# Four row tiles transposed within the weights' product, in four banks, and a bias product summed over chunks on VectorE

## The chip, the cores and the metric

The kernel runs on one core of a Trainium2 chip. The metric is the device time in microseconds (us) of one execution. Engines are named as the profile names them: PE is TensorE, DVE is VectorE, ACT is ScalarE, POOL is GpSimd, SP is SyncE, which here only issues DMA transfers.

## The reference

Two layers over a graph of N = 3327 rows and D = 512 columns. Everything is 32-bit floating point.

```
h  = relu(layernorm(x))
q, k, v = h Wq^T + bq, h Wk^T + bk, h Wv^T + bv
a  = q k^T / sqrt(512) + adj + adj
x  = x + softmax(a) v

h  = relu(layernorm(x))
A2 = adj + I,   s = diagonal(A2)^(-1/2)
x  = x + relu((s A2 s) (A2 h W1^T))
```

Only the preparation of the first layer's scores matters for the change. The kernel doesn't form q and k one by one: with M = Wq^T Wk / sqrt(512) and u = Wk^T bq / sqrt(512), the scores are (h M + u) h^T, up to a term that is constant along a row and drops out of the softmax.

## The kernel before

Rows are padded to 26 tiles of 128. The program is written with a tile framework that orders each engine's instructions by its own planner from the order of the text and adds the waits; from the score stage on an order written by hand is forced on PE, DVE, POOL and SP (`in_order`). On each engine instructions run in that order. So what moves in the text need not move equally far on every engine.

**Loading (L286 to L293).** Wq and Wk come in four chunks of 128 rows each, Wq on SP's queue and Wk on ACT's. From the second chunk on, an x tile follows on each of the two queues. The bias `bq_sb`, 128 x 4 values, comes after them on SP's queue (L293); all later x tiles, the adjacency blocks `g` and the stores of finished rows also go on SP's queue.

**The weights' product (L298 to L314).** Eight products of zeros into the bank `idle` (L302) run on PE while the first weights come. Then M: four banks `ps[r]`, 0 to 3, each summed over the four chunks `c`, so 16 products of 128x128 by 128x512 (L306); in 32-bit floating point each is two passes in the profile. ACT scales them out of PSUM in eight pieces (L311), and DVE forms one sum (L312) and three differences (`four_differences`, L181 to L183) that the products below need.

**Row tiles (`h_transposed`, L316).** The tiles are taken in four packs, `PACKS` = (0,4), (4,3), (7,3), (10,3), in the order `TURN` = 1, 2, 0, 3. A pack of n covers n tiles of the upper half and n of the lower half of the rows, so the first pack that is worked on has six tiles. For each tile: load x (`load_x`, L275, 11 buffers in turn), statistics on DVE (`norm`, L194 to L198), the power -1/2 on POOL (L200), the shift `nb` on DVE (L204), `ht` on ACT (L323, four buffers in turn), a store of `ht` (L324), four transposes on PE into one bank `tp` (L327), and the copies: all four blocks by ACT for an upper tile (L330), or two by ACT (L332) and two sums by DVE (L333, L334) for a lower one. `tp_bank` (L229) takes banks 6 and 7 in turn. After a pack's last tile DVE forms two more sums over the pack (L335, L336).

**The bias product (L370 to L375).** `pu`, in bank 4, holds Wk^T bq: for each of the four column blocks `r`, four products over the chunks `c`, each with a 128x128 block of Wk as weights and one column of `bq_sb` as the moving operand. DVE scales it into `u` (L375), which ACT adds to the projected rows (L352).

```
for r in range(DC):
    for c in range(DC):
        nc.tensor.matmul(pu[:, r : r + 1], w_k[c // 2][:, c % 2, r * P : (r + 1) * P], bq_sb[:, c : c + 1],
                         start=c == 0, stop=c == DC - 1)
```

**Projection (`project_q`, L338).** For a pack, two chains of seven products each (`Chain`, L231) between the blocks of M and the pack's `hp`, in the banks X (0, 1), Y (2, 3) and Z (4, 5), L347; results go to `qs` by ACT (L352) and DVE (L355) and are stored to DRAM (L362). The transposes of the next pack are woven in between by the planner.

**Afterwards** come the scores (L454), with the adjacency and the exponentials, and then the large products over the rows (L813 and others) of both layers. Their text is the same before and after.

Of the kernel before, what the change touches and what calls it, by code (L numbers as in the profile page):

```python
# [12 lines left out]
ALU = mybir.AluOpType  # L13
AX = mybir.AxisListType

P = 128
# [31 lines left out]
def graph_layers_kernel(  # L48
# [28 lines left out]
    nc = tc.nc  # L77
    N = out.shape[0]
    NP, D = x.shape
    DC = D // P  # L80
    NT = NP // P
    scale = 1.0 / math.sqrt(D)
    E = D // 2
# [22 lines left out]
    def half(k, shape, name):  # L106
        return arena.tile(shape, F32, name=name, tag=f"half{k}")

    def bank(k, name):
        return banks.tile([P, BW], F32, name=name, tag=f"bank{k}")  # L110
# [35 lines left out]
    ones = const.tile([P, 1], F32, name="ones")  # L146
# [9 lines left out]
    bq_sb = const.tile([P, DC], F32, name="bq_sb")  # L156
# [20 lines left out]
    def four_differences(b, first=0):  # L177

        if first == 0:
            yield nc.vector.tensor_sub(b[4], b[0], b[1])  # L180
        yield nc.vector.tensor_add(b[5], b[3], b[4])  # L181
        yield nc.vector.tensor_sub(b[6], b[1], b[3])
        yield nc.vector.tensor_sub(b[7], b[2], b[5])  # L183
# [7 lines left out]
    def norm(src):  # L191

        st = small.tile([P, 6], F32, name="st")
        nc.vector.bn_stats(st, src)  # L194
        mv = small.tile([P, 2], F32, name="mv")
        nc.vector.bn_aggr(mv, st)
        ve = small.tile([P, 1], F32, name="ve")
        nc.vector.tensor_scalar(ve, mv[:, 1:2], EPS, None, op0=ALU.add)  # L198
        rstd = small.tile([P, 1], F32, name="rstd")
        nc.gpsimd.tensor_tensor(rstd, ve, mhalf, op=ALU.pow)  # L200

        def bias():
            nb = small.tile([P, 1], F32, name="nb")
            nc.vector.scalar_tensor_tensor(nb, mv[:, 0:1], -1.0, rstd, op0=ALU.mult, op1=ALU.mult)  # L204
            return nb

        return rstd, bias
# [6 lines left out]
    TURN = (1, 2, 0, 3)  # L214
# [10 lines left out]
    def psum_ring(*ks):  # L225
        turn = itertools.cycle(ks)
        return lambda name: bank(next(turn), name)

    x_bank, y_bank, z_bank, tp_bank = psum_ring(0, 1), psum_ring(2, 3), psum_ring(4, 5), psum_ring(6, 7)  # L229
# [43 lines left out]
    def load_x(i, queue=nc.sync):  # L273
        xt = x_ring([P, D], "xt")
        queue.dma_start(xt, x[ROW[i] * P : (ROW[i] + 1) * P])  # L275
        return xt
# [3 lines left out]
    def blocks(slots, name):  # L280

        return [b[:, k] for b in (half(j, [P, 2, 2, E], name) for j in slots) for k in range(2)]

    w_q, w_k = ([half(k, [P, 2, D], name) for k in slots] for name, slots in (("wq", (0, 1)), ("wk", (2, 3))))

    first = {}  # L286
    for c in range(DC):
        for w, src, queue in ((w_q, wq, nc.sync), (w_k, wk, nc.scalar)):
            queue.dma_start(w[c // 2][:, c % 2], src[c * P : (c + 1) * P])
        if c > 0:  # L290
            for (_, i), queue in zip(order[2 * c - 2 : 2 * c], (nc.sync, nc.scalar)):
                first[i] = load_x(i, queue)
    nc.sync.dma_start(bq_sb, bq)  # L293
    M = blocks(range(4, 8), "M")
    u = const.tile([P, DC], F32, name="u")

# [3 lines left out]
    idle = bank(5, "idle")  # L300
    for _ in range(8):
        nc.tensor.matmul(idle[:, :P], zero, zero, start=True, stop=True)  # L302
    ps = [bank(k, "mm") for k in range(DC)]
    for c in range(DC):
        for r in range(DC):
            nc.tensor.matmul(ps[r], w_q[c // 2][:, c % 2, r * P : (r + 1) * P], w_k[c // 2][:, c % 2],  # L306
                             start=c == 0, stop=c == DC - 1)
    for r in range(DC):
        for z in range(2):
            turned = -scale if r < 2 and z == 0 else scale  # L310
            nc.scalar.mul(M[2 * (r // 2) + z][:, r % 2], ps[r][:, z * E : (z + 1) * E], turned)  # L311
    nc.vector.scalar_tensor_tensor(M[4], M[0], -1.0, M[1], op0=ALU.mult, op1=ALU.subtract)  # L312
    for _ in four_differences(M, 1):
        pass  # L314

    def h_transposed(k):  # L316

        a, n = PACKS[k]
        for _, i in (o for o in order if o[0] == k):
            xt = first.pop(i) if i in first else load_x(i)  # L320
            rstd, bias = norm(xt)
            ht = n_ring([P, D], "ht")
            nc.scalar.activation(ht, xt, AF.Relu, bias=bias(), scale=rstd)  # L323
            nc.sync.dma_start(rowd[0][ROW[i]], ht)  # L324
            pt = tp_bank("tp").rearrange("p (c e) -> p c e", c=DC)
            for c in range(DC):
                nc.tensor.transpose(pt[:, c], ht[:, c * P : (c + 1) * P], ident)  # L327
            w = slice((i % HALF - a) * P, (i % HALF - a + 1) * P)
            if i < HALF:
                nc.scalar.copy(hp[k][:, 0:2, :, w], pt.rearrange("p (a c) e -> p a c e", a=2))  # L330
            else:
                nc.scalar.copy(hp[k][:, 2, :, w], pt[:, 2:4])  # L332
                nc.vector.tensor_add(hp[k][:, 3, :, w], hp[k][:, 2, :, w], pt[:, 0:2])  # L333
                nc.vector.tensor_add(hp[k][:, 5, :, w], hp[k][:, 0, :, w], pt[:, 0:2])  # L334
        nc.vector.tensor_add(hp[k][:, 4], hp[k][:, 3], hp[k][:, 0])  # L335
        nc.vector.tensor_add(hp[k][:, 6], hp[k][:, 1], hp[k][:, 4])  # L336

    def project_q(k):  # L338
        a, n = PACKS[k]
        w = n * P  # L340

        qs = [half(8 + j, [P, 2, BW], "qs") for j in range(4)]

        def chain(o):
            def product(ps, name, start):
                for c in range(2):
                    nc.tensor.matmul(ps[:, :w], M[B[name]][:, c, o * P : (o + 1) * P], hp[k][:, A[name], c],  # L347
                                     start=start and c == 0, stop=c == 1, skip_group_check=True)

            def first(j, ps, sign):  # L350
                d = 2 * (j % 2) + o
                nc.scalar.activation(qs[j][:, o, :w], ps[:, :w], AF.Identity, bias=u[:, d : d + 1], scale=float(sign))  # L352

            def more(j, ps):
                nc.vector.tensor_add(qs[j][:, o, :w], qs[j][:, o, :w], ps[:, :w])  # L355

            def last():
                if o == 1:
                    for j in range(4):
                        y, z = divmod(j, 2)  # L360
                        i = ROW[y * HALF + a] * P
                        nc.sync.dma_start(qd[:, 2 * z : 2 * z + 2, i : i + w], qs[j][:, :, :w])  # L362

            Chain(product, first, more, last)

        for o in range(2):
            chain(o)

    h_transposed(TURN[0])
    pu = bank(4, "pu")  # L370
    for r in range(DC):
        for c in range(DC):
            nc.tensor.matmul(pu[:, r : r + 1], w_k[c // 2][:, c % 2, r * P : (r + 1) * P], bq_sb[:, c : c + 1],
                             start=c == 0, stop=c == DC - 1)
    nc.vector.tensor_scalar(u, pu[:, :DC], scale, None, op0=ALU.mult)  # L375
    for k, then in itertools.zip_longest(TURN, TURN[1:]):
        if then is not None:
            h_transposed(then)
        project_q(k)


# [170 lines left out]
    with in_order(*(e.engine for e in (nc.vector, nc.tensor, nc.gpsimd, nc.sync))):  # L552
# [9 lines left out]
        k = len(steps)  # L562
# [459 lines left out]
    def number_of(g, r, s, t):  # L1022
        return ((g * len(ORDER) + r) * 2 + s) * len(every) + t
# [5 lines left out]
    for g in range(3):  # L1029
        for n, r in enumerate(ORDER):  # L1030
            for t, e in enumerate(every):
                k = number_of(g, n, 0, t)
# [9 lines left out]
    for n, job in enumerate(jobs):  # L1042
        k = k0 + n * (k1 - k0) // len(jobs)
# [15 lines left out]
    k = number_of(0, 5, 1, 2)  # L1059
# [6 lines left out]
    k = number_of(1, 5, 1, 2)  # L1066
# [9 lines left out]
    for (n, s, t), its in {  # L1076
# [4 lines left out]
        for i, when in zip(its, (between, within)):  # L1081
            if i is not None:
                k = number_of(2, n, s, t)
# [8 lines left out]
    k = number_of(1, 4, 0, 0)  # L1092
# [480 lines left out]
```

## Time and profile before

| what | value |
|---|---|
| time, median of 3 runs | 2179.59 us (2177.32 to 2180.01) |
| profiled execution: its own time | 2178.22 us |
| profiled execution: span | 2176.4 us |
| PE busy | 2163.2 us (99%) |
| DVE busy | 1664.5 us (76%) |
| ACT busy | 238.4 us (11%) |
| first product of the score stage (L454) starts | 115.99 us |

The time of an execution is somewhat longer than its span, which runs from the first to the last instruction. PE busy counts pipelined products with modelled ends; a busy PE can still be working at a lower clock, which the profile shows as PEclk. In the chain of waits the last instruction is followed back to what released it, so its pieces add up to the span. In lists of groups, `x` is a count of records: two for a product in 32-bit floating point, one for a transpose. Line numbers are those of the kernel before.

### The profile page before, as it was taken

To read this page: it belongs to the slowest core of one execution; us is meant where nothing else is said; L and a number is where in the kernel's file an instruction comes from. 1 tells how busy PE (TensorE), PEld (TensorE's weight loads), DVE (VectorE), ACT (ScalarE), POOL (GpSimd) and SP (SyncE) were. 2 spreads that over 40 slices of the span, in tenths; PEclk is the share of its full clock that TensorE was granted. 3 is DMA by queue.
4 is the path that set the end of the run, shared out by engine and by line. 5 is a ranking of instruction groups with operands and counts; after the bars stand their busy time and mean duration, and the time that the engine had idled before them with its cause. 6 is when DMAs were issued, how large, how long until landed. Compare 5 with 4: busy or idle time off the path is not lost.

```text
span 2176.4 us, 21093 instructions
## 1 busy us (share of the span) xinstructions
PE 2163.2 (99%) x6424; PEld 1197.1 (55%) x6424; DVE 1664.5 (76%) x3250; ACT 238.4 (11%) x363; POOL 49.0 (2%) x60
## 2 busy tenths in 40 slices
PE   9999999999999999999999999999999999999998
PEld 6555555455555555555454555555666655555555
DVE  6369888888886698886778778887676667778686
ACT  5312111121110000000000000000011100000011
POOL 2000000000000000000111000000000000000000
PEclk9999999999999999999999999999999999999999
DMA  8568888889989899888787889986646468756685
GB/s 290 177 222 308 294 298 287 294 290 310 321 290 298 291 377 331 287 296 304 259 304 263 308 277 370 320 303 219 207 145 200 142 202 276 254 188 212 218 305 194
DMA packets 300374, 583.68 MB, mean 268 GB/s; under 512 B 34518, under 2 KB 168028, under 8 KB 300252
## 3 DMA queue, kind: packets, MB, share of 16 engines
q1 hardware_dynamic: 265102, 512.76, 69.4%
q10 hardware_dynamic: 35150, 69.48, 8.7%
q8 instruction: 53, 0.87, 0.2%
q14 instruction: 69, 0.57, 0.1%
HBM read 414.28 MB, written 167.85 MB: 267 GB/s over the span
## 4 chain that ended last, share of the span: by engine, by line
PE 95%; DVE 3%; DMA 1%; issue 1%; ACT 0%; POOL 0%; DVEq 0%; POOLq 0%
PE p L813 54%; PE Y L454 13%; PE Z L454 7%; PE p L805 5%; PE p L905 4%; PE pw L966 3%; PE X L454 3%; PE Y L347 2%; PE Z L347 1%; PE mm L306 1%; DMA part<-sum 1%; PE tp L327 1%; DVE part L173 1%; PE pt L995 1%; PE X L347 0%
## 5 line engine op out<-in xcount | busy, mean ns | idle before, releaser
L813 PE MATMUL p<-part,b 128*128 128x448 f32 (+1 forms) x3528 | 1261.5, 513 | 0.3 <-DVE part L174 0.2
L813 PEld LDWEIGHTS p<-part,b 128*128 128x128 f32 x3528 | 668.1, 190 | 534.7 <-issue 284.7
L454 PE MATMUL Y<-qt,hp 128*128 128x448 f32 (+1 forms) x832 | 308.2, 513 | 0.3 <-DVE g L466 0.3
L173 DVE TENSOR_TENSOR part<-part 128x896 f32<-128x896 f32 (+1 forms) x252 | 257.0, 1020 | 65.7 <-DMA part<-p 24.0
L454 PEld LDWEIGHTS Y<-qt,hp 128*128 128x128 f32 x832 | 157.7, 190 | 134.3 <-issue 72.3
L454 PE MATMUL Z<-qt,hp 128*128 128x384 f32 (+1 forms) x416 | 162.5, 513 | 0.0
L175 DVE TENSOR_TENSOR part<-part,part 128x448 f32<-128x448 f32 (+1 forms) x219 | 129.5, 591 | 14.9
L174 DVE TENSOR_TENSOR part<-part,part 128x448 f32<-128x448 f32 (+1 forms) x219 | 129.4, 591 | 7.2
L805 PE MATMUL p<-part,b 128*128 128x448 f32 (+1 forms) x336 | 124.2, 513 | 0.0
L454 PEld LDWEIGHTS Z<-qt,hp 128*128 128x128 f32 x416 | 78.8, 190 | 67.4 <-issue 37.2
L458 DVE SCALAR_TENSOR_TENSOR g<-g,Y 128x384 f32<-128x384 f32 (+1 forms) x156 | 91.5, 587 | 31.3 <-PE Y L454 28.6
L805 PEld LDWEIGHTS p<-part,b 128*128 128x128 f32 x336 | 63.7, 190 | 53.5 <-issue 31.2
L841 ACT COPY part<-p 128x384 f32<-128x384 f32 (+1 forms) x33 | 16.6, 502 | 657.5 <-PE p L813 542.1
L454 PE MATMUL X<-qt,hp 128*128 128x384 f32 (+1 forms) x208 | 81.1, 512 | 0.0
L461 ACT ACTIVATE g<-g 128x768 f32<-128x768 f32 (+1 forms) x48 | 43.0, 896 | 347.8 <-DVE g L458 278.6
L905 PE MATMUL p<-w,ct 128*128 128x512 f32 x136 | 61.8, 594 | 0.5 <-DVE part L917 0.5
L842 DVE TENSOR_TENSOR part<-p,part 128x384 f32<-128x384 f32 (+1 forms) x33 | 19.3, 585 | 51.6 <-PE p L813 50.9
L454 PEld LDWEIGHTS X<-qt,hp 128*128 128x128 f32 x208 | 39.5, 190 | 33.1 <-issue 19.3
L200 POOL TENSOR_TENSOR rstd<-ve,mhalf 128x1 f32<-128x1 f32 x52 | 43.0, 830 | 567.9 <-DVE ve L198 538.7
L966 PE MATMUL pw<-w,rows 128*128 128x256 f32 x208 | 53.6, 380 | 0.8 <-DVE rows L956 0.8
L896 DVE TENSOR_TENSOR job<-job 128x896 f32<-128x896 f32 (+1 forms) x52 | 52.9, 1018 | 0.0
L466 DVE TENSOR_TENSOR g<-g,Z 128x384 f32<-128x384 f32 (+1 forms) x52 | 30.5, 586 | 26.8 <-PE Z L454 26.4
(176 smaller groups left out, 1697.6 us busy)
## 6 DMA issues: line engine op xcount, KB each, us to landing
part<-sum SPq DMA_DIRECT2D x104, 448.0 KB, 5.0
part<-p SPq DMA_DIRECT2D x91, 448.0 KB, 6.0
part<-sum SPq DMA_DIRECT2D x104, 384.0 KB, 3.7
part<-p SPq DMA_DIRECT2D x91, 384.0 KB, 4.4
part<-in_adjT_dram SPq DMA_DIRECT2D x78, 448.0 KB, 4.9
b<-row SPq DMA_DIRECT2D x234, 128.0 KB, 4.7
part<-in_adjT_dram SPq DMA_DIRECT2D x78, 384.0 KB, 3.5
g<-in_adjT_dram SPq DMA_DIRECT2D x52, 448.0 KB, 4.4
```

The costliest lines, as they stand in the source:

```text
L173: yield nc.vector.tensor_add(o[:, 0:2], g[:, 0:4:3], g[:, 1:2].to_broadcast([P, 2, g.shape[-1]]))
L174: yield nc.vector.tensor_add(o[:, 2], o[:, 1], g[:, 0])
L175: yield nc.vector.tensor_add(o[:, 3], o[:, 2], g[:, 2])
L200: nc.gpsimd.tensor_tensor(rstd, ve, mhalf, op=ALU.pow)
L347: nc.tensor.matmul(ps[:, :w], M[B[name]][:, c, o * P : (o + 1) * P], hp[k][:, A[name], c], start=start and c == 0, stop=c == 1, skip_group ...
L454: nc.tensor.matmul(ps[:, :wd], h_of(self.t, name, k), qt[B[name]][:, k], start=start and k == 0, stop=k == 1, skip_group_check=True)
L458: nc.vector.scalar_tensor_tensor(a[n], a[n], 2.0, ps[:, :wd], op0=ALU.mult, op1=ALU.add if sign > 0 else ALU.subtract)
L805: yield nc.tensor.matmul(ps[("p2", "p3", "p4", "p8")[k]][:, :w], b[:, z], a[:, 0, y], start=k == 3, stop=True)
L813: yield nc.tensor.matmul(ps[r][:, :w], b[:, i], m, start=self.t == 0, stop=self.t == PAIRS - 1 and r in ("p1", "p5", "p6", "p7"))
L896: nc.vector.tensor_add(self.a, self.a, self.b)
L905: nc.tensor.matmul(ps, cts[s][y][d][:, k * P : (k + 1) * P], w[d], start=d == 0, stop=d == DC - 1)
L966: nc.tensor.matmul(ps, a, W[B[name]][:, c], start=new and c == 0, stop=c == 1, skip_group_check=True)
```

## The change

Three things change, all in the first stretch of the program.

The six tiles of the first pack are now made by a generator. Its first four tiles are drawn in the text between chunk 2 and chunk 3 of the weights' product, the other two after M and its differences. For this pack the transposes take the banks 6, 7, 4, 5 in turn; the later packs keep 6 and 7.

The bias is first multiplied into the rows of Wk on DVE: `weighed`, 128x512, is the sum over the chunks of a chunk of Wk times its column of the bias, one instruction for each chunk. Then four products of a 128x128 block of `weighed` with the column `ones` give `pu`, now in bank 0, in place of sixteen.

The bias is loaded on ACT's queue after the second chunk of Wk, in place of SP's queue after the last chunk.

```diff
@@ loading
     for c in range(DC):
         for w, src, queue in ((w_q, wq, nc.sync), (w_k, wk, nc.scalar)):
             queue.dma_start(w[c // 2][:, c % 2], src[c * P : (c + 1) * P])
+        if c == 1:
+            nc.scalar.dma_start(bq_sb, bq)
         if c > 0:
             for (_, i), queue in zip(order[2 * c - 2 : 2 * c], (nc.sync, nc.scalar)):
                 first[i] = load_x(i, queue)
-    nc.sync.dma_start(bq_sb, bq)
@@ h_transposed
-    def h_transposed(k):
+    def h_transposed(k, tp_bank=tp_bank):
...
                 nc.vector.tensor_add(hp[k][:, 5, :, w], hp[k][:, 0, :, w], pt[:, 0:2])
+            yield
         nc.vector.tensor_add(hp[k][:, 4], hp[k][:, 3], hp[k][:, 0])
@@ the weights' product; the scaling into M and the differences follow it as before
     ps = [bank(k, "mm") for k in range(DC)]
+    begun = h_transposed(TURN[0], psum_ring(6, 7, 4, 5))
+    weighed = half(12, [P, D], "weighed")
     for c in range(DC):
+        if c == DC - 1:
+            for _ in itertools.islice(begun, 4):
+                pass
+        if c == 0:
+            nc.vector.tensor_scalar(weighed, w_k[0][:, 0], bq_sb[:, 0:1], None, op0=ALU.mult)
+        else:
+            nc.vector.scalar_tensor_tensor(weighed, w_k[c // 2][:, c % 2], bq_sb[:, c : c + 1], weighed,
+                                           op0=ALU.mult, op1=ALU.add)
         for r in range(DC):
             nc.tensor.matmul(ps[r], w_q[c // 2][:, c % 2, r * P : (r + 1) * P], w_k[c // 2][:, c % 2],
                              start=c == 0, stop=c == DC - 1)
@@ after M and its differences
-    h_transposed(TURN[0])
-    pu = bank(4, "pu")
+    for _ in begun:
+        pass
+    pu = bank(0, "pu")
     for r in range(DC):
-        for c in range(DC):
-            nc.tensor.matmul(pu[:, r : r + 1], w_k[c // 2][:, c % 2, r * P : (r + 1) * P], bq_sb[:, c : c + 1],
-                             start=c == 0, stop=c == DC - 1)
+        nc.tensor.matmul(pu[:, r : r + 1], weighed[:, r * P : (r + 1) * P], ones, start=True, stop=True)
     nc.vector.tensor_scalar(u, pu[:, :DC], scale, None, op0=ALU.mult)
```

## The prediction

> **What bounds the kernel now.** I read the page first, then the waits of TensorE, then the chain of waits over the first 60 us, then the table by stage.
>
> ```profile
> PE 2163.2 (99%) x6424; PEld 1197.1 (55%) x6424; DVE 1664.5 (76%) x3250; ACT 238.4 (11%) x363; POOL 49.0 (2%) x60
> ...
> PE 95%; DVE 3%; DMA 1%; issue 1%; ACT 0%; POOL 0%; DVEq 0%; POOLq 0%
> ```
>
> TensorE is busy 99% of the span and holds 95% of the chain that ended last. The change touches only the first 30 us, so the question is what TensorE loses there: passes that can go, waits, and passes at a lower clock. Its waits over the whole run are few:
>
> ```profile
> PE tp L327 <- ACT hp L330: 0.7, 1, 0.7
> PE tot L507 <- DVE acc L510: 0.6, 1, 0.6
> ```
>
> The longest is in the stretch that is changed; all others lie after 600 us, but for 0.14 us at 54.8. After 31 us TensorE runs almost without a hole, so a microsecond saved before that should reach the end. The chain of the first stretch (start, length, what; x counts passes):
>
> ```profile
> 4.92 14.82 PE mm L306 x32
> 19.74 0.87 PE tp L327 x8
> 20.61 3.47 PE pu L373 x32
> 24.08 0.91 PE tp L327 x4
> 24.99 0.02 issue
> 25.01 0.59 ACT hp L330
> 25.61 0.04 issue
> 25.65 1.97 PE tp L327 x8
> 27.62 1.47 PE Y L347 x2
> 29.09 0.85 PE tp L327 x4
> 29.95 1.16 PE Y L347 x2
> 31.10 0.65 PE X L347 x2
> 31.75 0.87 PE tp L327 x8
> ```
>
> To be seen here: the 16 one-column products `pu` cost 3.47 us; then 0.66 us of waiting for ACT's copy; and the same shapes cost twice as much from 24 to 31 us as after it (eight transposes 1.97 against 0.87, two passes of a product 1.47 against 0.65). The table by stage (us, PE busy, PEld, DVE, ACT, POOL, PEclk, DMA share, GB/s) says why:
>
> ```profile
> 23.00:24.00 1.00, 1.00 (x11) 1.00 (x11) 1.00 (x4) 0.00 (x0) 0.00 (x0) 1.00 0.95 283
> 24.00:25.00 1.00, 0.97 (x5) 0.57 (x4) 0.53 (x4) 0.00 (x0) 0.00 (x0) 0.51 0.64 225
> 27.00:28.00 1.00, 1.00 (x4) 0.72 (x4) 1.00 (x8) 1.00 (x2) 0.00 (x0) 0.50 0.86 301
> 31.00:32.00 1.00, 1.00 (x7) 0.69 (x6) 0.06 (x1) 0.75 (x2) 0.55 (x1) 1.00 0.00 0
> ```
>
> The granted clock (PEclk) halves at about 24.0 and returns at about 30.9.
>
> **What the Trainium skill says.** "TensorE: Matmul & The Clock Gate", Part 1: the clock is set by TensorE's activity in free-running windows of 3413 ns; a window without it brings half clock. The trace agrees in length: 24.0 to 30.9 is two windows, and the one before them, 20.6 to 24.0, holds nothing but `pu`. The same page, Part 4, says that transposes do not count as activity in the same way; that fits the second window, 24.0 to 27.4, which held only transposes and the wait. No view shows how little activity is too little: 27.4 to 30.9, about 70% product passes, brought full clock back.
>
> **The change, part by part.** The program's new order on each engine can be read without running it; from the thirteenth row tile's transposes on, TensorE's order is the old one.
>
> 1. *`pu` from 16 products to 4.* 32 passes at 3.47/32 = 0.108 us become 8: 3.47 - 0.87 = **2.60 us less**, all on TensorE's path.
>
> 2. *The wait at 24.99 goes: 0.66 us less.* With two banks in turn the fifth tile needs the third's, whose copy on ACT had only begun. Now the first four tiles have a bank each and are copied while chunk 3 runs, so the fifth finds its bank free.
>
> 3. *The half clock goes, if no window is empty.* Against the rows at full clock: 0.91-0.44, 1.97-0.87, 1.47-0.65, 0.85-0.44, 1.16-0.65 = **3.31 us less**. The new order is: chunks 0 to 2 of the product, 16 transposes (1.75), chunk 3 (3.43), two tiles (0.87), `pu` (0.87), one tile, three products with M. The longest stretch without wide products is 21.3 to 23.9, 2.6 us, shorter than a window.
>
> 4. *Four tiles ahead of chunk 3.* TensorE works in order, so chunk 3 and all behind it now wait for these `ht`. The first is needed at 16.3 (19.74 less chunk 3's eight passes at 0.43), the fourth at 17.6. In the run before, ACT made the same four from 13.59 on, because the first `nb` stood behind the fifth tile's statistics on VectorE's queue; in the new order it stands behind the third's. I work out about 10.3 to 13.7 us: nearly 4 us of slack for the fourth, cost nothing. The transposes only move.
>
> 5. *`weighed`, four VectorE instructions.* The row of the same form (the M sum at L312, 128x512) takes 0.69 us, 0.60 from start to start: 2.4 us between 6 and 12 us, where VectorE stood idle 6.4 us until the first x tile, then 1.1 and 0.8. Bounds: 0.3 to 0.9 each; nothing on the path while the slack of point 4 holds.
>
> 6. *The bias load goes from SP's queue (8.49) to ACT's third place (about 1.6).* The x tile, chunk 2 and all later loads on ACT stand behind it: one issue, about 0.4 us; its 2 KB are hardly traffic. x tiles issued at that time land 5.4 to 5.8 us later, so 7.4 is its upper bound, about 6.0 my value. VectorE's first instruction, and the statistics behind it, wait for it: the x tiles come at 7.3 to 7.5 anyway. In the round of eight DMA semaphores chunk 2 of Wk is now the ninth load and waits for the first to land: it leaves at 4.3 instead of 2.12. Bound: nothing to 2.2 us; nothing, since an x tile in front of it keeps the queue busy until about 7.3 and TensorE needs chunk 2 at 12.8. SP loses one issue (0.33 us).
>
> 7. *What is late next.* ACT now copies the four tiles and makes two more `ht` around M: copies 0.48 + 0.27 twice, `ht` at 0.72, M's eight at 0.30. M ends near 22.9 instead of 20.4, the first copy after it near 23.4. The seventh tile shares that tile's bank, so TensorE waits from about 23.1 to 23.5: **0.4 us**. Then three products to about 25.8, and the eighth tile's bank waits for VectorE: the M sum, three differences, statistics of tiles that arrive at 20 to 24 us and two adds (0.33 each) end near 26.9: **1.1 us**. Some 0.3 us of small waits may follow. Sum 1.8, bounds 0.5 to 3. The seven-product chains then run as before; `u`, at about 27.7, is needed by ACT at 28.4.
>
> Sum: -2.60 - 0.66 - 3.31 + 1.8 = **-4.8 us** of the span; a second laying-out of each engine's new order with these durations gave -4.6. I take -4.6: span 2171.8. The profiled execution took 2178.22 for a span of 2176.4, 1.8 beside it, so 2173.6 for this one. The median of the three runs, 2179.59, is 1.4 higher. The profiled run had two half-clock windows; where the free-running window falls otherwise, a run before may have one, and lose about 1.7 us less. So against the median I take off 0.4: a gain of 4.2, **2175.4 us**. 0.2% is 4.36 us, about what a measurement of this kernel can tell from no change: the forecast lies just inside.
>
> **The rivals.**
>
> *A: one or two windows still fall short* (chance 0.25). For: 21.3 to 23.9 and 25.8 to 27.8 hold no wide product, and the threshold is unknown. Against: each window holds at least 0.8 us of product passes. One window costs 0.2 to 1.3 us net (part of it falls into the waits of point 7), two cost 1.9: gain 2.3 to 3.5, 2176 to 2177.3.
>
> *B: the new waits do not come* (0.2). If x tiles land early enough that VectorE is done by 25.8, only 0.5 us of point 7 is left: 6.57 - 0.5, about 6 us gained, 2173.5. For: VectorE has gaps before 20 us. Against: DMA share was 1.0 until 20 us, so tiles don't come sooner.
>
> *C: slower: TensorE stands in front of chunk 3* (0.05). Place: the transposes between chunk 2 and 3; everything is queued behind them. Price: a microsecond for each microsecond by which the fourth `ht` comes after 17.6. With the bias at 6.0 it comes at 13.7; the gain is used up if VectorE starts 8.4 us later, at about 14.4, and slower by 0.2% needs 18.8. Only a bias load held behind the x traffic would do it; rows of that time (5.8 us at most) speak against it. At a bias landing of 19: some 2184.
>
> **How the numbers follow.** The main case has 0.5: gains 3.5 to 5.2, centre 4.2, so 2174.4 to 2176.1. Runs before differ by 2.7 us among themselves, which widens each case by about 1.4. Over 0.2% faster is all of B and a little under half of the main case: 0.42; within 0.2% the rest of it and A: 0.53; slower 0.05. Range: from B with its spread, 2172.8, to A's worse end with its spread, 2178.6.
>
> **What would show it.** Right: in the chain after, `pu` at about 0.87 us; no 0.66 us wait on ACT in front of a tile, but about 0.4 and 1.1 us, the latter on VectorE's adds; PEclk 1.0 throughout 20 to 32 us; the first product of the next stage (L454 before) starting 4 to 5 us earlier than 115.99. The fourth `ht` before 16 us shows point 4 right. Wrong: PEclk at 0.5 again after 21 us (A), a wait on VectorE or ACT ahead of the 16 transposes (C), or a lead at 45 us that is gone at 116, which would mean that something beside TensorE paced those stages.

## The result and the profile after

| | before | after |
|---|---|---|
| median of the timed runs | 2179.14 us (18 runs, 2175.35 to 2183.09) | 2175.52 us (18 runs, 2174.13 to 2178.04) |
| ratio after/before | | 0.9984, 95% interval 0.9977 to 0.9991 |
| profiled execution | 2178.22 us, span 2176.4 | 2175.3 us, span 2173.4 |
| first product of the score stage starts | 115.82 us | 112.36 us |

The kernel is 3.6 us faster, with an interval of 2.0 to 5.0 us (0.0009 and 0.0023 of 2179). A second comparison of the same two kernels, given below, has 0.9985. (115.82 and 112.36 are the first records of that product in TensorE's timeline; the 115.99 given earlier for the kernel before is the same product in another view.)

In the profile after, first TensorE's busy time on the page, and its waits (engine, what waited, for whom, then total us, times, longest us):

```profile
PE 2158.9 (99%) x6400; PEld 1192.8 (55%) x6400; DVE 1667.4 (77%) x3254; ACT 238.1 (11%) x363; POOL 47.3 (2%) x60
PE tp L315 <- ACT hp L318: 1.8, 1, 1.8
PE tp L315 <- ACT ht L311: 0.2, 1, 0.2
```

24 TensorE records are gone, as the change says, and TensorE is busy 4.3 us less. The old wait of 0.7 us for a copy of ACT is gone too, but a longer one for the same kind of copy is there. Where it lies is seen in TensorE's timeline (start, length, then the engine, line and form; the bracket is the idle time ahead of the group and what ended it):

```profile
16.86 3.60 PE L371 MATMUL mm<-wk,wq 128*128 128x512 f32 x8
20.29 0.60 PE L315 MATMUL tp<-ident,ht 128*128 128x128 f32 x4
21.14 0.66 PE L315 MATMUL tp<-ident,ht 128*128 128x128 f32 x4 [0.24 <-ACT ht L311]
21.69 1.05 PE L386 MATMUL pu<-ones,weighed 128*128 128x1 f32 x8
24.50 0.66 PE L315 MATMUL tp<-ident,ht 128*128 128x128 f32 x4 [1.76 <-ACT hp L318]
25.00 3.79 PE L336 MATMUL Y<-hp,M 128*128 128x384 f32 x6
```

Chunk 3 (the eight `mm` passes) runs behind the four early tiles. `pu` has shrunk to 8 passes. Then TensorE stands for 1.76 us ahead of the seventh tile, and the six passes of Y take 3.79 us, where six such passes at 54.06 take 2.10. The table by stage (us, PE busy, PEld, DVE, ACT, POOL, PEclk, DMA share, GB/s) has the reason:

```profile
24.00:25.00 1.00, 0.50 (x5) 0.50 (x6) 1.00 (x5) 1.00 (x3) 0.00 (x0) 1.00 1.00 358
26.00:27.00 1.00, 1.00 (x3) 0.66 (x2) 1.00 (x3) 1.00 (x2) 0.28 (x1) 0.50 0.85 260
29.00:30.00 1.00, 1.00 (x9) 0.87 (x7) 0.94 (x2) 0.67 (x2) 0.00 (x0) 1.00 1.07 404
```

One window of half clock is left, from 25.24 to 28.65 us in the clock's record, where before had two, 24.03 to 30.85.

**A measure that leaves most of the start out.** The moment at which the clock first rises differs from run to run: 6.96 us in the profiled run before, 4.76 after, and with it chunk 2 of the weights' product ended a microsecond earlier (15.27 for 16.30). So the experiments are compared by the *lead*: the time from the end of the product's 24th pass (three chunks) to the first score product. It was 99.5 before and 97.1 after, a gain of 2.4 us in the trace. (The lead still depends on the start in part; the two runs of e4, at the end of the experiments, show how.) From that product to the end, runs took 2060.1 to 2063.4 us without any pattern in what had been changed: that is the noise of the time.

### The profile page after: what moved, and what is told of

Its sections match the earlier page's. It is cut to its first block, busy times and chain, and to the rows that moved or that the text cites. A ratio compares the mean times of both kernels' runs of the same rounds, so it can differ in the third digit from the quotient of the medians.

```text
span 2173.4 us, 21053 instructions
## 1 busy us (share of the span) xinstructions
PE 2158.9 (99%) x6400; PEld 1192.8 (55%) x6400; DVE 1667.4 (77%) x3254; ACT 238.1 (11%) x363; POOL 47.3 (2%) x60
## 4 chain that ended last, share of the span: by engine, by line
PE 93%; DVE 4%; DMA 2%; issue 1%; ACT 0%; POOL 0%; SPq 0%; ACTq 0%; DVEq 0%; POOLq 0%
PE p L826 54%; PE Y L467 13%; PE Z L467 6%; PE p L818 5%; PE p L918 4%; PE pw L979 3%; PE X L467 3%; PE Y L336 2%; PE Z L336 1%; DMA part<-sum 1%; DVE part L173 1%; PE pt L1008 1%; PE X L336 0%; DMA rows<-row 0%; PE tp L315 0%
## 5 line engine op out<-in xcount | busy, mean ns | idle before, releaser
L854 ACT COPY part<-p 128x384 f32<-128x384 f32 (+1 forms) x33 | 16.6, 502 | 657.4 <-PE p L826 570.7
```

## The experiments

All but the first two rows were timed in five rounds against the kernel before, whose medians in those rounds were 2178.36 (beside e1, e2, e4, e5), 2179.17 (e3, e6, e7, e8) and 2178.87 us (the last four rows). The ratio is the one on record, and not simply the quotient of two medians. "Half windows" are stretches of 3.41 us at half clock between 15 us and the score stage, in the profiled run.

| kernel | median us | ratio to before, 95% | lead us | half windows |
|---|---|---|---|---|
| before, profiled run | 2179.14 | | 99.5 | 2 |
| after | 2175.52 | 0.9984, 0.9977 to 0.9991 | 97.1 | 1 |
| e1, bias part alone | 2179.54 | 1.0004, 0.9996 to 1.0013 | 99.2 | 2 |
| e2, tiles' part alone | 2176.12 | 0.9985, 0.9977 to 0.9994 | 97.6 | 1 |
| e3, more `ht` buffers | 2176.24 | 0.9987, 0.9979 to 0.9996 | 97.3 | 1 |
| e4, seventh and eighth tile in banks 4, 5 | 2174.11 | 0.9976, 0.9966 to 0.9985 | 94.2 | 0 |
| e5, bias loaded late | 2176.29 | 0.9988, 0.9982 to 0.9995 | 98.5 | 1 |
| e6, two banks for the first pack | 2175.13 | 0.9985, 0.9978 to 0.9993 | 95.1 | 0 |
| e7, e3 and e4 together | 2176.05 | 0.9990, 0.9981 to 0.9998 | 95.0 | 0 |
| e8, two useless wide products | 2177.49 | 0.9993, 0.9985 to 1.0001 | 99.6 | 1 |
| e9, before with `pu` 128 columns wide | 2177.51 | 0.9995, 0.9987 to 1.0003 | 98.8 | 0 |
| e10, e6 and e4 together | 2175.36 | 0.9985, 0.9978 to 0.9992 | 98.0 | 1 |
| after, again | 2175.79 | 0.9985, 0.9978 to 0.9992 | 97.1 | 1 |
| e4, again | 2173.91 | 0.9981, 0.9973 to 0.9990 | 96.2 | 1 |

TensorE's timeline lets a lead be taken apart. *Idle* is the time within the lead in which TensorE runs nothing, *half clock* is half of its busy time at half clock, and *passes* is the rest, which is what its passes take at full clock. The ten profiled runs with the short `pu` and nothing added have 93.0 to 93.4 us of passes, so the account is good to some 0.2 us.

| kernel | lead us | passes | idle | half clock |
|---|---|---|---|---|
| before | 99.5 | 95.6 | 0.8 | 3.1 |
| e1 | 99.2 | 93.2 | 3.3 | 2.7 |
| e2 | 97.6 | 95.7 | 0.1 | 1.7 |
| after | 97.1 | 93.2 | 2.1 | 1.7 |
| e4 | 94.2 | 93.4 | 0.8 | 0 |
| e4, again | 96.2 | 93.2 | 1.3 | 1.7 |
| e8 | 99.6 | 95.0 | 2.9 | 1.7 |
| e9 | 98.8 | 96.2 | 2.7 | 0 |

### Each part alone: e1 and e2

e1 is the kernel before with `weighed`, four `pu` products and the early bias load; the tiles stay where they were.

```diff
+        if c == 1:
+            nc.scalar.dma_start(bq_sb, bq)
-    nc.sync.dma_start(bq_sb, bq)
...
-        for c in range(DC):
-            nc.tensor.matmul(pu[:, r : r + 1], w_k[c // 2][:, c % 2, r * P : (r + 1) * P], bq_sb[:, c : c + 1],
-                             start=c == 0, stop=c == DC - 1)
+        nc.tensor.matmul(pu[:, r : r + 1], weighed[:, r * P : (r + 1) * P], ones, start=True, stop=True)
```

> The kernel before with the bias product alone changed: weighed on VectorE, four products for pu, the bias loaded early on ACT's queue; all row tiles stay behind the weights' product and use two banks. Theory (each part has its own share): pu falls from 3.47 to about 0.87 us and the empty stretch between wide products shrinks from 7.9 to about 5.3 us, so one half-clock window in place of two; the old wait of about 0.7 us on ACT's copy stays. From the end of the third chunk to the first score product about 97 us (before 99.7), time 2176 to 2177. Rival (the tiles' move is worth nothing, or its gain was eaten by its own waits): the same time as the changed kernel, 2175.5, and as short a stretch, 97.1.

e2 is the changed kernel with the sixteen `pu` products and the late bias load of before, and without `weighed`.

```diff
...
-        nc.tensor.matmul(pu[:, r : r + 1], weighed[:, r * P : (r + 1) * P], ones, start=True, stop=True)
+        for c in range(DC):
+            nc.tensor.matmul(pu[:, r : r + 1], w_k[c // 2][:, c % 2, r * P : (r + 1) * P], bq_sb[:, c : c + 1],
+                             start=c == 0, stop=c == DC - 1)
```

> The changed kernel with the bias product as it was: sixteen products for pu, bias loaded last on SP's queue; the four tiles still stand in front of chunk 3 in four banks. Theory: pu costs 3.47 us again, but it now runs while ACT and VectorE work through M and the copies, so the wait in front of the seventh tile (1.76 us in the changed kernel) goes and pays back part; against it the stretch without wide products is 5 us or more and brings at least one half-clock window. From the end of the third chunk to the first score product 97.5 to 98.5 us; time 2176.5 to 2177.5. Rival (the gain is pu's passes alone): 99.7 us and 2179.

e1 gained nothing: 1.0004, lead 99.2, two half windows. e2 has nearly the whole gain: lead 97.6, 0.5 us behind the full change. TensorE's timeline of e1:

```profile
20.22 0.95 PE L379 MATMUL pu<-ones,weighed 128*128 128x1 f32 x8
21.03 0.63 PE L334 MATMUL tp<-ident,ht 128*128 128x128 f32 x4
22.34 0.66 PE L334 MATMUL tp<-ident,ht 128*128 128x128 f32 x4 [0.68 <-ACT hp L337]
25.09 1.11 PE L334 MATMUL tp<-ident,ht 128*128 128x128 f32 x4 [2.09 <-DVE hp L341]
```

Most of the 2.6 us that `pu` no longer takes stand in the bracket of the fourth line. The bank that this tile needs is given free by VectorE's adds (L341). In VectorE's timeline those come at 24.29 to 24.95, behind the sum of M and its three differences (21.23 to 24.3):

```profile
23.69 0.68 DVE L183 TENSOR_TENSOR M<-M 128x512 f32<-128x512 f32 x1
24.62 0.41 DVE L341 TENSOR_TENSOR hp<-hp,tp 128x256 f32<-128x256 f32 x1
```

In the kernel before, TensorE was inside `pu` until 23.9 during that same work. e2 shows the other half in its chain of waits:

```profile
21.26 3.47 PE pu L380 x32
24.73 0.77 PE tp L314 x4
25.50 3.35 PE Y L335 x6
```

The long `pu` ends at 24.7, and the seventh tile follows without a wait: the bank that it needs had been copied by 23.3. In the full change the same copy ends at 24.45 (ACT's timelines, first e2, then the full change):

```profile
22.62 0.65 ACT L317 COPY hp<-tp 128x512 f32<-128x512 f32 x1
23.79 0.66 ACT L318 COPY hp<-tp 128x512 f32<-128x512 f32 x1
```

So `pu`'s 3.47 us lay beside work of ACT and VectorE that ended late as well. From before to e1 the passes fall by 2.4 us and the idle time grows by 2.5; from e2 to the full change they fall by 2.5 and it grows by 2.0. Taking `pu` down was worth 0.3 to 0.5 us of lead. e2's own gain has no passes in it: it is 0.7 us of idle time and one of the two half windows.

### Where the new wait comes from: e3, e4, e7

The seventh tile shares a bank with the fifth, whose copy waits on ACT. In the trace after, the fifth `ht` began at 18.82 only: its buffer was still being stored to DRAM until 18.7. e3 gives the fifth to eighth tile buffers of their own.

```diff
-            ht = n_ring([P, D], "ht")
+            late = order.index((k, i)) - 4
+            ht = half(8 + late, [P, D], "ht") if 0 <= late < 4 else n_ring([P, D], "ht")
```

> The changed kernel with eight ht buffers for the first eight tiles (four of them in space that the projection uses later) in place of four. Theory (the fifth ht waited until 18.8 for the first tile's ht buffer, which its store frees, and that store stands behind five x tiles and an adjacency block in the DMA queue; this delayed M and all copies on ACT): the fifth ht comes before 16.5, M and the first copy after it come about 1 us earlier, and the wait in front of the seventh tile falls from 1.76 to about 0.7 us; 2174.6. Rival (ACT's queue alone is the delay: two ht and four copies around M): the wait stays at 1.5 us or more, 2175.5.

The buffers let ACT make those four `ht` at 16.30 to 19.5, and the wait stayed, 1.77 us. ACT's timeline of e3 shows why:

```profile
20.91 0.84 ACT L312 ACTIVATE ht<-xt,nb,rstd 128x512 f32<-128x512 f32 x1
21.62 1.22 ACT L377 ACTIVATE M<-mm 128x256 f32<-128x256 f32 x4
22.68 0.86 ACT L312 ACTIVATE ht<-xt,nb,rstd 128x512 f32<-128x512 f32 x1
23.39 1.25 ACT L377 ACTIVATE M<-mm 128x256 f32<-128x256 f32 x4
24.44 0.67 ACT L319 COPY hp<-tp 128x512 f32<-128x512 f32 x1
```

ACT had more finished by then, but its order puts two further `ht` and the eight pieces of M ahead of the copy (L319). With the buffers free, the wait is one for ACT's queue. (In the changed kernel itself the chain of waits behind the seventh tile goes back through ACT to a store of `ht`, 14.43 to 19.96. Taking that store out of the chain was not enough.) So e4 goes round the wait: in the second pack the first two tiles, the seventh and eighth of the whole, get banks 4 and 5.

```diff
-            for _ in h_transposed(then):
+            rings, turn = (psum_ring(4, 5), tp_bank), itertools.count()
+            for _ in h_transposed(then, (lambda name: rings[next(turn) > 1](name)) if k == TURN[0] else tp_bank):
```

> The changed kernel with the first two tiles of the second pack in banks 4 and 5, long copied by then, in place of 6 and 7. Theory (the 1.76 us in front of the seventh tile are a wait for its bank, whose copy stands behind M on ACT, and the eighth tile's later wait is for VectorE's adds on the bank of the sixth): both go, the seventh and eighth tile follow pu at once, the first M product starts at about 23.5 in place of 25.0; 1.0 to 1.5 us less, 2174.2. Rival (something else paces this stretch, M on ACT or the sums on VectorE): the wait moves in front of the first M product, 2175.5.

TensorE's timeline of e4:

```profile
22.36 0.95 PE L386 MATMUL pu<-ones,weighed 128*128 128x1 f32 x8
23.18 0.63 PE L315 MATMUL tp<-ident,ht 128*128 128x128 f32 x4
23.86 2.20 PE L336 MATMUL Y<-hp,M 128*128 128x384 f32 x6
```

There is no wait ahead of the seventh tile, Y's six passes take 2.20 us in place of 3.79, and the lead falls to 94.2. In this run the passes that the short `pu` saves are gained in full: 93.4 us of passes, 0.8 idle, no half clock. e7 puts e3's buffers on top of e4.

> The changed kernel with eight ht buffers and with the second pack's first two tiles in banks 4 and 5. Theory: the seventh and eighth tile wait for nothing, and the first M product starts as soon as the fifth tile is copied, near 22.5; 1.5 us less than the changed kernel, 2174. Rival (VectorE's sums pace what follows, whatever comes before): no better than with either alone.

It did not add to e4: lead 95.0, with waits of 0.71, 0.26 and 0.82 us for ACT and others, as the planner orders ACT's work anew when `ht` may start earlier.

### What the four banks and the early bias load do: e6 and e5

e6 leaves the first pack on banks 6 and 7.

```diff
-    begun = h_transposed(TURN[0], psum_ring(6, 7, 4, 5))
+    begun = h_transposed(TURN[0])
```

> The changed kernel with the first pack's transposes in banks 6 and 7 alone. The planner then puts the third and fourth tile between the products of chunk 3. Theory (four banks are not what brings the gain, because a copy takes 0.5 us and a product of chunk 3 lasts 0.86): no difference beyond 0.5 us, 2175.5. Rival (the banks matter): the third tile waits for ACT's copy of the first and holds chunk 3, 0.6 us or more in two waits, 2176.5.

It was as fast as the full change (0.9985), with a lead of 95.1 in a profiled run that started late (the clock rose at 6.87 us). With two banks the tiles can't all be transposed at once, and chunk 3's passes went in between them, 17.02 to 22.5 us: two waits of 1.0 and 0.94 us came, but no window was left without enough wide passes. That is this one run: over the timed runs the mean clock is no higher than the full change's (0.999 in 9 of 16 runs, against 22 of 39; one half window takes 0.0008 off it). The four banks are not where the gain is from.

e5 puts the bias load back on SP's queue, behind the x tiles.

```diff
-        if c == 1:
-            nc.scalar.dma_start(bq_sb, bq)
+    nc.sync.dma_start(bq_sb, bq)
```

> The changed kernel with the bias load back at the end of the loads on SP's queue; weighed and four products stay. Theory (nearly 4 us of slack stand between the fourth ht and its transposes, and the planner puts weighed behind the fifth tile's statistics): the fourth ht comes at about 16 in place of 15.2, TensorE is held by 0 to 0.5 us ahead of chunk 3, 2175.5 to 2176.2. Rival (all of VectorE's statistics hang on the bias, as in case C of the prediction): TensorE waits 2 us or more ahead of chunk 3, 2178 or more.

This is the prediction's case C made real. Its price was small:

```profile
17.26 3.60 PE L370 MATMUL mm<-wk,wq 128*128 128x512 f32 x8
22.34 0.63 PE L314 MATMUL tp<-ident,ht 128*128 128x128 f32 x4 [1.05 <-DVE nb L204]
28.31 1.28 PE L314 MATMUL tp<-ident,ht 128*128 128x128 f32 x8 [2.12 <-DVE hp L321]
```

No bracket stands at chunk 3: VectorE had done the first two statistics at 7.43 to 9.1 and made `weighed` behind them (13.20 to 16.6). What was late were the tiles behind chunk 3, and the lead is 1.4 us longer than in the full change. The ratio, 0.9988, can't be told from that of the full change: the intervals overlap.

### The clock: e8, e9 and e10

If TensorE's activity in a window decides, wide products in the empty stretch should keep the clock up. e8 adds two useless ones behind `pu`.

```diff
+    warm = bank(1, "warm")
+    for r in range(2):
+        nc.tensor.matmul(warm, w_q[0][:, 0, :P], w_k[r][:, 0], start=True, stop=True)
```

> The changed kernel with two wide products without use (128x128 by 128x512, 1.7 us at full clock) behind pu, in a bank that is free by then; they fill the wait of 1.76 us in front of the seventh tile. Theory of the clock (a window with hardly a wide product brings half clock): the windows between 20 and 28 us hold wide products now, PEclk stays 1.0 in more runs, and the first three M products take 1.9 us, not 3.6; time the same or up to 1 us less. Rival (the clock falls for another reason, or the half clock was hidden behind VectorE anyway): PEclk at 0.5 for one window as before, and the two products cost up to 1.7 us where they delay what follows.

They cost more than they brought: the lead is 99.6, with 1.8 us more of passes and 0.7 us more of idle time than the full change. A wait of 2.33 us for ACT's `ht` came behind them (25.47), and the half window came one window later. Activity put in front of a wait did not shorten it here; the planner's order changed with it, too.

e9 asks the question of the kernel before: `pu`'s 32 passes keep their number and their time, but each has 128 columns of work in place of one.

```diff
...
-            nc.tensor.matmul(pu[:, r : r + 1], w_k[c // 2][:, c % 2, r * P : (r + 1) * P], bq_sb[:, c : c + 1],
-                             start=c == 0, stop=c == DC - 1)
+            nc.tensor.matmul(pu[:, r * 128 : (r + 1) * 128], w_k[c // 2][:, c % 2, r * P : (r + 1) * P],
+                             bq_sb[:, c : c + 1].to_broadcast([P, 128]), start=c == 0, stop=c == DC - 1)
...
```

> The kernel before, its sixteen pu products kept, with the bias column repeated over 128 columns as the moving operand: the same 32 passes of about 0.108 us, now with 128 columns of work each. In the text they stand after two row tiles, as they stood in TensorE's order before; behind them the planner draws tiles and first products in a somewhat different order. Theory (one-column passes count for little as TensorE's activity, so a window filled with them is followed by half clock): the window of pu no longer brings half clock; at most one half-clock window is left between 20 and 32 us instead of two, lead from the third chunk to the first score product about 97.5 to 98.5 (99.5 before), time ratio about 0.999. Rival (the half clock comes from the transposes and waits around pu, not from pu's narrow passes): two half-clock windows between 23 and 31 us as before, lead 99 to 100, ratio 1.000.

TensorE's timeline of e9:

```profile
19.84 3.74 PE L376 MATMUL pu<-bq_sb,wk 128*128 128x128 f32 x32
24.70 1.06 PE L327 MATMUL tp<-ident,ht 128*128 128x128 f32 x8 [0.68 <-DVE nb L204]
27.15 1.06 PE L327 MATMUL tp<-ident,ht 128*128 128x128 f32 x8 [1.39 <-DVE hp L334]
```

`pu` takes as long as before, there are waits of 0.68 and 1.39 us, and yet the clock did not fall: the record has 1.0 from 5.57 to 2169.6 us, where TensorE has nothing left to do. All 13 timed runs have a mean clock of 0.999, where the 57 runs of before beside them have 0.997 or 0.998 in 51 cases. (A run at 0.999 can hold one half window, as e3's profiled run does, but not two.) So one-column passes do not count as activity, or hardly. On the clock the theory's statement holds; its lead was 0.3 us too low. The lead fell by 0.7 us only, and by its interval the time can't be told from before's (0.9995, upper end 1.0003), though the median is 1.4 us lower. The table has the reason: 3.1 us of half clock are gone and 1.9 us of idle time have come, so part of what the full clock saved went into waits. The planner's order behind `pu` also changed somewhat, so the 0.7 us isn't the clock's alone.

e10 joins e6 and e4.

> The changed kernel with only banks 6 and 7 for the first pack, and banks 4 and 5 for the second pack's first two tiles. Theory (the wait of the seventh tile for ACT's copy is what is left to gain, and four banks for the first pack aren't needed): no wait of over 0.3 us between 21 and 26 us, the one of about 1.0 us inside chunk 3 stays, no half clock after 20 us, lead 94 to 95, ratio 0.9975. Rival (the copies on ACT are late wherever the bank is, so the wait only comes at another tile): a wait of 0.7 to 1.8 us between 22 and 27 us, lead 95 to 97, ratio 0.9985.

Neither statement holds as a whole: the ratio is the rival's, the cause is another one. The planner put the statistics of one early tile late on VectorE, TensorE stood 3.02 us inside chunk 3 waiting for `nb`, and half clock followed from 21.28 to 24.70. The wait behind `pu` was gone, as the theory had it, but the lead was 98.0: the gains of two versions do not add where the planner orders each anew.

### After and e4 once more

> The changed kernel, unaltered, for a comparison with the version with banks 4 and 5 on the same chip. If the comparison of the first runs holds: lead 97 (96.5 to 97.7), one half-clock window, a wait of 1.7 us for ACT at about 23 us, ratio 0.9984 (0.9977 to 0.9991). If what was seen before hung on where the clock's window fell: no half-clock window or two of them, lead 95.4 or 98.8.

> The version with banks 4 and 5 for the second pack's first two tiles, once more, beside the changed kernel on the same chip. If it is better for the reason given (no wait for the copy of the shared bank, and no half clock): lead 94 to 95, no half-clock window, ratio 0.9970 to 0.9982, about 1.5 to 3 us below the changed kernel. If its first result was luck with the clock's window: one half-clock window, lead 95.5 to 97, level with the changed kernel.

The changed kernel repeated itself closely (lead 97.11, a wait of 1.76 us, one half window, 0.9985). e4 was again the lowest, 2173.91, but its profiled run had a wait of 0.92 us ahead of Y and one half window, so its lead was 96.2, not 94.2. Both statements on it hold in part: the version is faster, and some of the 94.2 was luck. The luck lay in the start. TensorE ended its third chunk at 16.47 us in the first run and at 15.33 in the second, because the clock rose at 7.31 and at 4.44. ACT did not move with it: its fifth `ht` waits until the store of the first has landed, and began at the same time in both (first run, then second):

```profile
18.17 0.81 ACT L311 ACTIVATE ht<-xt,nb,rstd 128x512 f32<-128x512 f32 x1 [0.36 <-DMA row<-ht]
18.26 0.81 ACT L311 ACTIVATE ht<-xt,nb,rstd 128x512 f32<-128x512 f32 x1 [1.60 <-DMA row<-ht]
```

In the second run TensorE came early, found ACT no further, waited, and lost a half window as well: there an early rise of the clock lengthened the lead. The leads of e4's first run, e6 and e7 (rise at 6.87 to 7.31 us) are thus likely too good beside those of the other changed versions (4.21 to 5.68). Before and e1 (6.96, 6.51) can be set beside each other, and so can e2 and the full change (4.32; 4.76 and 5.24). Before's run had the late start, so the gain of 2.4 us in lead may well be too small; the medians have 3.6 and, the second time, 3.1.

At like starts, 15.33 against 15.28 and 15.53, e4's lead is 0.9 us shorter than the full change's. Against the changed kernel on the same chip it is 1.9 us lower by the medians, 21 and 13 runs; by resampling these runs, the difference lies between 2.9 lower and 0.5 higher. With the first runs of both added (39 and 22) it is 1.7 us, 0.5 to 2.6, though these come from rounds in which before's medians differed by 0.8. I take e4 as the better version, by an amount that is near the limit of what can be told.

## Why the prediction was right, and where it was not

The forecast was 2175.4 us and the measured median 2175.52, within 0.2% of before but faster. The near meeting of the two numbers is luck in part: the prediction started from a median of 2179.59, 0.45 above the later one, and forecast a gain of 4.2 where 3.6 was measured. The steps behind it did worse than the sum. By the prediction's numbering:

1. *`pu`, 2.60 us less, "all on TensorE's path": wrong.* The passes went (3.47 to some 0.9 us), but e1 and e2 value this at 0.3 to 0.5 us, because 2.5 and 2.0 us of idle time came in their place. The step failed where it took a busy engine for a bounding one: the chain of waits before ran through `pu`, but VectorE and ACT were nearly as late, which the prediction saw (point 7) and did not set against point 1.
2. *The old wait of 0.66 us goes: right.* The fifth tile finds its bank free; the wait of 0.24 us that is left is the sixth's, for its `ht`.
3. *The half clock goes, 3.31 us: half right.* One of two windows is left. In it Y's six passes took 3.63 us in the chain where 1.94 is full speed (the six at 54.23), so 1.69 was not gained. The condition, no window without wide products, was reasoned without the 1.76 us wait: the window before the half clock, 21.83 to 25.24, held 0.24 us of wide passes, 0.49 of transposes, 0.92 of `pu` and the wait. The prediction had at least 0.8 us of product passes in each window. This is rival A's event, in two of two profiled runs.
4. *Four `ht` in time: right.* They were done at 15.2 us (1.5 later than worked out), and no wait stands ahead of the 16 transposes or chunk 3. The slack was not nearly 4 us, though: TensorE came early, and the fourth tile's transposes began at 16.4, so 1.2 us were left.
5. *`weighed` costs nothing: right.* 0.49, 0.73, 0.75 and 0.75 us on VectorE, 0.3 us more in all than forecast.
6. *The bias load: right.* VectorE's first wait ended at 6.43, forecast 6.0. Case C did not come, and e5 shows that a late bias hits the tiles behind chunk 3, not chunk 3.
7. *New waits, 1.8 us in sum: right in sum, wrong in place.* The seventh tile waited 1.76, not 0.4. M ended on ACT at 24.0, not 22.9, since ACT's fifth `ht` waited until 18.82 for its buffer and ACT made one more `ht` between M's pieces (22.03); and TensorE was there 0.4 us earlier. The prediction had no term for that buffer. (In e2 the same `ht` began at 17.64; why the store landed later in the full change was not tried.) The 1.1 us for VectorE at the eighth tile did not appear: the wait and the half clock ahead of it gave VectorE the time.

By terms the lead has 2.4 us fewer passes, 1.4 less of half clock and 1.3 more of idle time: -2.4 in all, where the forecast had -2.6 of passes, -3.3 of half clock and +1.1 of waits (-0.66 and +1.8), -4.8 in all. The gain by the medians, 3.6 us with its interval of 2.0 to 5.0, holds both the forecast's 4.2 and the trace's 2.4, so it can't decide between them. The first score product came 3.5 us earlier, not the 4 to 5 that the prediction had named, and 1.0 of that is the earlier start.

On the clock the prediction leaned on the Trainium skill, "TensorE: Matmul & The Clock Gate", Part 1, for windows of 3413 ns, and the runs agree: of the ten half stretches between 15 us and the score stage in the 14 traces, eight are 3.41 us long, and the two of before and e1 are 6.83. It also took from Part 4 that transposes do not count in the same way. Here they counted at full clock: in e7 a window with 0.61 us of wide passes and 1.94 of transposes was followed by full clock, in e4's second run one with 0.97 and 0.66 was followed by half, each with 0.7 to 0.8 us of one-column passes beside them. The measurement decides: it was `pu`'s one-column passes, and then the waits, that left the windows empty.

## What to carry to other kernels

An engine that is busy 99% of the span can still be in step with two others: before counting an instruction's time as a gain, ask when the next buffer that TensorE needs would be free without it. Do one part of a change alone; here the part that removed the most TensorE work was worth almost nothing as long as the wait behind it stood, and the part that only moved work was worth nearly all. With that wait shortened (e4), more of the removed passes counted: in its second run the lead is 1.4 us under that of e2. Where a wait follows a run of tiny passes, shorten the wait (here by another PSUM bank) rather than fill it.

## What the runs showed of the hardware

The surprise was how sharply activity separates the windows. For each window at full clock between about 12 and 55 us, in all 14 profiled runs, I summed TensorE's passes of 128 columns or more and its transposes, each counted until the next instruction began:

```
half clock follows   0.1 and 0.2 (before and e2, with 3.3 and 3.2 us of one-column passes)
                     0.5 (e10)  0.7 (after)  0.9 (after again)  1.0 (e3)  1.1 (e8)  1.3 (e5, e1)  1.6 (e4 again)
full clock follows   2.3, 2.4 (e9)  2.4 (e5, e6)  2.5 (e3, e4, e7) and all that are fuller
```

The windows can be placed because in each trace every change of the clock, the last fall after 2167 us included, lies within 0.01 us of a grid of 3.4133 us counted from the first rise. The limit lies between 1.63 and 2.31 us of 3.41 in these runs, with one-column passes left out; e4's second run had 0.68 us of them on top of its 1.63, and fell all the same. At half clock more is needed by this count: 1.9 us (e1) and 2.7 us of transposes (before) did not bring full clock back, 3.3 us did. That transposes and products weigh alike was not tried by itself. The waits decide together with the place of the grid: the 1.76 us wait of the changed kernel came in both its profiled runs and left a window with too little both times, while e4 had such a window only in the run with the wait of 0.92 us.
